# Low part of the attention rows and the last residual on GpSimd, means subtracted as they are: a macaron block on one Trainium2 core

## The chip, the cores and the metric

The kernel runs on one core of one Trainium2 chip. A core has five engines that work side by side, each through its own queue of instructions in order: TensorE (PE, with its weight loads shown apart as PEld), VectorE (DVE), ScalarE (ACT), GpSimd (POOL) and SyncE (SP), which here issues the DMAs. The metric is the device time of one execution in microseconds; lower is better. The time before is the median of three executions.

## The reference

One "macaron" layer on x of shape 8 x 1024 x 256: half a feed-forward block, an attention with relative positions (16 heads of 16 channels), and the same half feed-forward block again, each on a layer-normalized input and added to x.

```python
x = x + 0.5 * ffn(layernorm(x))
x = x + attention(layernorm(x))      # with a relative shift of the positions
x = x + 0.5 * ffn(layernorm(x))

def ffn(x):        return tanh(x @ W1 @ W2 @ W3 + bias)
def attention(x):
    content = einsum('bihd,bjhd->bhij', q + u_bias, k)
    pos     = relative_shift(einsum('bihd,jhd->bhij', q + v_bias, p))
    attn    = softmax((content + pos) * scale)
    return (attn @ v) @ Wo + bo
```

The change touches the layer norms (the mean that is subtracted) and the last two lines of work: the projection by Wo and the second feed-forward block.

## The kernel before

**Prologue** (to about 300 us). For each of eight groups of 128 positions it normalizes x, runs the first feed-forward block and computes queries, keys and values. The class Stats holds the statistics: ends() aggregates mean and variance on VectorE, negates the mean into a tile n (L272) and makes the reciprocal deviation r on GpSimd (rsqrt, L105 and L106); apply() (L287) computes (x + n) * r on GpSimd.

**Attention loop** (to about 2850 us). The scores are cut into 64 units: four groups of query rows by 16 heads. A unit has 16 steps, one for each of its query rows; a unit's sums over the values (L971, 128 matmuls) stand at the start of the next. step(T) writes out by hand the order in which each engine gets its work:

- TensorE: the first half of the scores of step T+2 (L1029), the subtraction of the maximum for step T (L959), a third of the second half (L1037), the transposed maxima of step T+1 (L945), the rest of the second half (L1043).
- VectorE: the maximum over each half (L934, twice), the two merged (L940: two f16 tiles of SBUF), the maximum over rows (L947).
- ScalarE: the exponentials of both halves (L963, twice), and a diagonal tile dg that holds the row maxima for L959 (L952).
- GpSimd: one copy a step (L225) that rearranges queries for the next unit, 16 for a unit. They are not paced: GpSimd takes them as soon as its queue reaches them and their tiles are free. The first of a unit waits until TensorE has read the tile for the last time.

PSUM holds three buffers of each half of the scores.

**Output work inside the loop.** When the 16 heads of a group of rows are done, the eight batches of that group are put through post_ops, one after the other, while the next group's scores run; so 24 of the 32 are done in the loop. posts(T) takes the next piece at the end of a step, and a number beside each piece says how many steps pass before the next one. The tiles of this use have one buffer (nb is 1). The pieces of one batch are: load; norm (GpSimd multiplies the heads' sums by the reciprocal denominators, L773); hi1 (ScalarE rounds num to f16 into the first part of hl, L777) and lo1 in the same step (what was lost by rounding, into the second part of hl, L780); projres one step later (12 matmuls with Wo, L786, and VectorE's residual, L798); ln (statistics and the negated mean, L112, L114, L117) and apply (GpSimd, L105, L106, L816) in one step; four steps later trans (L825, L830, L831); then ffn (L786, L837, and the tanh L838); fin (half of the tanh added to xr, L847); store. A batch takes exactly as many steps as a unit has, so each unit in such a stretch has one batch's pieces in the same places.

**The end** (from about 2850 us). The last group's eight batches go through post_ops with eight buffers (nb is 8) from ln on, staged by hand. There fin has two forms: for the first five batches ScalarE halves the tanh (L844) and GpSimd adds (L845); for the last three VectorE does both (L847).

Of the kernel before, what the change touches and what calls it, by code (L numbers as in the profile page):

```python
# [10 lines left out]
F32 = mybir.dt.float32  # L11
AF = mybir.ActivationFunctionType
ALU = mybir.AluOpType
# [3 lines left out]
P = 128  # L17
NB = 8
# [25 lines left out]
def macaron_kernel(  # L44
# [23 lines left out]
    nc = tc.nc  # L68
# [35 lines left out]
    def rsqrt(r, var):  # L104
        nc.gpsimd.tensor_scalar(r, var, 1.0, EPS, ALU.mult, ALU.add)  # L105
        nc.gpsimd.tensor_tensor(r, r, mhalf[:, : r.shape[1]], ALU.pow)  # L106

    def stats_dve(pool, xt, n, nm):
        st = pool.tile([P, n, 6], F32, tag="st" + nm, name="st" + nm)
        mv = pool.tile([P, n, 2], F32, tag="mv" + nm, name="mv" + nm)  # L110
        for b in range(n):
            nc.vector.bn_stats(st[:, b, :], xt[:, b, :])  # L112
        for b in range(n):
            nc.vector.bn_aggr(mv[:, b, :], st[:, b, :])  # L114
        r = pool.tile([P, n], F32, tag="r" + nm, name="r" + nm)
        nm_ = pool.tile([P, n], F32, tag="n" + nm, name="n" + nm)
        nc.vector.tensor_scalar_mul(nm_, mv[:, :, 0], -1.0)  # L117
        return nm_, r, mv

# [6 lines left out]
    class UnitSet:  # L128
        def __init__(self, pool, n):
            def t(name, shape):  # L130
                return pool.tile(shape, F16, tag=f"{name}{n}", name=f"{name}{n}")

            self.qc = t("qc", [KC, UT, 4, 32])
            self.q = t("q", [KR, UT + 1, NI * NB, 2])
            self.k = t("k", [KC, NI, 4, P])
            self.pg = t("pg", [KR, GW])
# [93 lines left out]
    if True:  # L230
        p2 = early.enter_context(tc.tile_pool(name="p2", bufs=2, side="right"))
# [25 lines left out]
        class Stats:  # L257
            def __init__(self, nm, xt):
                self.nm, self.xt = nm, xt
                self.st = p2.tile([P, NB, 6], F32, tag="st" + nm, name="st" + nm)  # L260
                self.mv = p2.tile([P, NB, 2], F32, tag="mv" + nm, name="mv" + nm)
                self.r = p2.tile([P, NB], F32, tag="r" + nm, name="r" + nm)
                self.n = p2.tile([P, NB], F32, tag="n" + nm, name="n" + nm)

            def rows(self, lo, hi):
                for b in range(lo, hi):
# [2 lines left out]
            def ends(self):  # L269
                for b in range(NB):  # L270
                    nc.vector.bn_aggr(self.mv[:, b, :], self.st[:, b, :])
                nc.vector.tensor_scalar_mul(self.n, self.mv[:, :, 0], -1.0)  # L272
                rsqrt(self.r, self.mv[:, :, 1])

            def again(self):
# [8 lines left out]
            def apply(self, tag):  # L284
                xn = p2.tile([P, NB, D], F32, tag=tag, name=tag, bufs=1)
                for b in range(NB):
                    nc.gpsimd.tensor_scalar(  # L287
                        xn[:, b, :], self.xt[:, b, :], self.n[:, b : b + 1],
                        self.r[:, b : b + 1], ALU.add, ALU.mult,
                    )  # L290
                return xn

# [125 lines left out]
        def key(xT, ks, m, h):  # L418
            ps = pst.tile([P, 512], F32, tag="t", name="kk")
            three(ps, wk16, xT, m, h)  # L420
            pv = ps.rearrange("p (b n) -> p b n", b=4)
            hi, lo = (ks[:, m, hl, 4 * h : 4 * h + 4] for hl in range(2))
            bc = bkk[:, m : m + 1]

            def one():
                nc.scalar.activation(hi, pv, AF.Identity, bias=bc)
                nc.vector.scalar_tensor_tensor(
                    out=lo, in0=pv, scalar=bc, in1=hi, op0=ALU.add, op1=ALU.subtract
                )

            return one
# [229 lines left out]
        for I in range(NI - 2, -2, -1):  # L661
# [39 lines left out]
            for n in range(4):  # L701
                q = query(xTb, cvst[(I + 1) % 2], n % 2, n // 2)
                k = key(xTb, ks, n % 2, n // 2)
# [24 lines left out]
    def load_rows(t, src, rg):  # L728
        for e, r in ((0, 16 * rg), (1, 64 + 16 * rg)):
            nc.sync.dma_start(  # L730
                t[:, e, :], src.rearrange("(k r) c -> k r c", r=P)[:, r : r + 16]
            )
# [21 lines left out]
    def post_ops(rg, b, sb, nb, pm, pt_, t):  # L754
        def new(name, shape, tag=None, dt=F32):
            t[name] = sb.tile(shape, dt, tag=tag or name, name=name, bufs=nb)
            return t[name]

        def load():
            num = new("num", [P, 2, 2 * P])  # L760
            den = new("den", [P, 2, 2 * P])
            for hh in range(2):
                hs = slice(8 * hh, 8 * hh + 8)
                nc.sync.dma_start(num[:, hh, :], h_d[rg, hs, 0:DH, b])
                nc.sync.dma_start(
                    den[:, hh, :],
                    r_d[rg, hs, b : b + 1, :].broadcast_to([8, DH, 2 * P]),
                )
            xr = new("xr", [P, 2, D])
            load_rows(xr, x1c_d[b], rg)  # L770

        def norm():
            nc.gpsimd.tensor_tensor(t["num"], t["num"], t["den"], ALU.mult)  # L773

        def hi1():
            new("hl", [P, 2, 2, 2 * P], dt=F16)
            nc.scalar.copy(t["hl"][:, 0], t["num"])  # L777

        def lo1():
            nc.vector.tensor_tensor(t["hl"][:, 1], t["num"], t["hl"][:, 0], ALU.subtract)  # L780

        def prod(ps, hl, w, tk, extra):
            n = 0
            for k in range(2):
                for a, c in ((0, 0), (1, 0), (0, 1)):
                    mm(  # L786
                        ps[:, tk, :], hl[:, a, k, tk * P : (tk + 1) * P], w[:, c, k, :],
                        start=n == 0, stop=n == 5 and not extra,
                    )
                    n += 1  # L790

        def proj():
            t["ps"] = pm.tile([P, 2, D], F32, tag=pt_, name="wops")
            for tk in range(2):
                prod(t["ps"], t["hl"], wo16, tk, False)

        def res():
            nc.vector.scalar_tensor_tensor(  # L798
                out=t["xr"], in0=t["ps"], scalar=1.0 / WS, in1=t["xr"], op0=ALU.mult,
                op1=ALU.add,  # L800
            )

        def projres():
            proj()
            res()

        def ln():
            if nb > 1:
                res()
            t["nm"], t["r"], t["mv"] = stats_dve(sb, t["xr"], 2, f"p{b % nb}")  # L810

        def apply():
            rsqrt(t["r"], t["mv"][:, :, 1])
            xn = new("pn", [P, 2, D])
            for k in range(2):
                nc.gpsimd.tensor_scalar(  # L816
                    xn[:, k, :], t["xr"][:, k, :], t["nm"][:, k : k + 1],
                    t["r"][:, k : k + 1], ALU.add, ALU.mult,
                )

        def trans():
            t["ps"] = pm.tile([P, 2, 2 * P], F32, tag=pt_, name="ptp")
            for c in range(2):
                for tk in range(2):
                    nc.tensor.transpose(  # L825
                        t["ps"][:, c, tk * P : (tk + 1) * P],
                        t["pn"][:, tk, c * P : (c + 1) * P], ident,
                    )
            new("pT", [P, 2, 2, 2 * P], "hl", F16)
            nc.scalar.copy(t["pT"][:, 0], t["ps"])  # L830
            nc.vector.tensor_tensor(t["pT"][:, 1], t["ps"], t["pT"][:, 0], ALU.subtract)  # L831

        def ffn():
            t["ps"] = pm.tile([P, 2, D], F32, tag=pt_, name="pff")
            for tk in range(2):
                prod(t["ps"], t["pT"], w16, tk, True)
                mm(t["ps"][:, tk, :], ones16, brow, start=False, stop=True)  # L837
            nc.scalar.activation(  # L838
                new("pth", [P, 2, D], "pn"), t["ps"], AF.Tanh, scale=1.0 / WS
            )  # L840

        def fin():
            if nb > 1 and b < NB - 3:
                nc.scalar.mul(t["pth"], t["pth"], 0.5)  # L844
                nc.gpsimd.tensor_tensor(t["xr"], t["xr"], t["pth"], ALU.add)  # L845
                return
            nc.vector.scalar_tensor_tensor(  # L847
                out=t["xr"], in0=t["pth"], scalar=0.5, in1=t["xr"],
                op0=ALU.mult, op1=ALU.add,
            )  # L850

        def store():
            store_rows(out[b], t["xr"], rg)

        return [
            (load, 4), (norm, 2), (hi1, 0), (lo1, 1), (projres, 0), (ln, 0), (apply, 4),
            (trans, 1), (ffn, 0), (fin, 1), (store, 1),
        ]

# [221 lines left out]
    num = [ttile(f"tn{k}", [P, NB, 2 * P]) for k in range(2)]  # L1081
# [152 lines left out]
```

## Time and profile before

| what | value |
|---|---|
| median of three executions | 2954.7 us (2951.74 to 2957.57) |
| the profiled execution | 2962.17 us, span of its profile 2960.5 us |
| granted TensorE clock, mean | 0.984; 1.00 through the loop |
| L934 (maxima), 2048 times | 687 ns each |
| L940 (merge of maxima), 1024 times | 224 ns at least, 226 median, 903 at most |
| L225 on GpSimd, two groups of 507 | 658 and 687 ns each |
| L780 (low part on VectorE), 24 times | 692 ns each |
| L773 (a product on GpSimd), 24 times | 1287 ns each |
| L845 (the addition on GpSimd), 5 times | 1267 ns median |
| L644 (a low part on GpSimd in the prologue), 4 times | 1155 ns each |

In the lines of the profile, out<-in names tiles, then come shapes and types, and a count. A line of the timeline begins with the start in us from the span's start and the time that the merged instructions took together; a bracket at its end is the time that the engine sat idle just before, with what ended that wait. A busy share over the whole span says little here, since the three stages have different limits; so the loop is read by units and steps.

### The profile page before, as it was taken

The page shows a single profiled execution, that of the slowest core. Times are in us where ns is not written, and L with a number is a line of the kernel's source. Part 1 is how long each engine was busy: PE and PEld are TensorE (multiplying, and loading weights), DVE is VectorE, ACT ScalarE, POOL GpSimd, SP SyncE. Part 2 cuts the span into 40 slices and gives each one's busy share as a digit, 9 for nine tenths or more (in the row PEclk, how much of TensorE's full clock was granted, in tenths as well). Part 3 has the DMA queues.
Part 4 walks back from the last instruction along what each step waited for, and adds up shares of the span by engine and source line. Part 5 has one row for each costly group of instructions (what it writes and reads, how often), then busy time and mean ns, then how long its engine had stood idle before and what let it go on. Part 6 is the DMA issues. An engine that isn't in the chain of part 4 may idle for free.

```text
span 2960.5 us, 157394 instructions
## 1 busy us (share of the span) xinstructions
PE 2835.1 (96%) x71212; PEld 2345.5 (79%) x71212; DVE 2188.1 (74%) x5001; ACT 1666.0 (56%) x3551; POOL 991.9 (34%) x1498
## 2 busy tenths in 40 slices
PE   7987999999999999999999999999999999999985
PEld 4755888888888888888888888888888888888874
DVE  7885777777777877877777787777777777777774
ACT  3655555555555655555555565556655556555552
POOL 8874222222222332332222332332222233232204
PEclk8999999999999999999999999999999999999997
DMA  4555322222223333322223323322223232222232
GB/s 146 185 164 177 87 69 68 65 66 67 67 68 76 85 85 86 85 76 68 66 66 78 84 81 86 83 70 70 70 70 78 82 87 81 83 68 65 67 88 70
DMA packets 333397, 250.63 MB, mean 85 GB/s; under 512 B 118885, under 2 KB 317142, under 8 KB 332246
## 3 DMA queue, kind: packets, MB, share of 16 engines
q1 hardware_dynamic: 332726, 240.56, 28.9%
q8 instruction: 558, 9.14, 1.3%
q14 instruction: 113, 0.93, 0.1%
HBM read 177.44 MB, written 62.78 MB: 81 GB/s over the span
## 4 chain that ended last, share of the span: by engine, by line
PE 83%; DVE 6%; DMA 2%; ACT 1%; issue 1%; SPq 1%; POOL 0%; ACTq 0%; DVEq 0%; POOLq 0%
PE s L1029 22%; PE s L1043 17%; PE av L971 15%; PE s L959 15%; PE s L1037 6%; DVE m L934 3%; PE mps L945 2%; PE pff L786 1%; DVE m L940 1%; PE wops L786 1%; DMA xr<-x1c_d 1%; ACT dg L952 1%; PE vv L467 1%; PE qq L454 1%; PE ptp L825 1%
## 5 line engine op out<-in xcount | busy, mean ns | idle before, releaser
L963 ACT ACTIVATE eT<-s 128x512 f32<-128x512 f32 x2048 | 1111.7, 594 | 992.3 <-PE s L959 990.7
L934 DVE TENSOR_REDUCE m<-s 128x128 f16<-128x512 f32 x2048 | 1406.3, 687 | 163.2 <-PE s L1029 30.6
L225 POOL TENSOR_SCALAR qc<-raw 48x256 f16<-48x256 f16 x507 | 328.6, 658 | 1229.0 <-PE s L1043 1191.4
L959 PE MATMUL s<-dg,many 128*128 128x512 f16 x2048 | 607.9, 378 | 33.0 <-ACT dg L952 33.0
L947 DVE TENSOR_REDUCE nm<-mps 128x1 f32<-128x128 f32 x1024 | 296.0, 289 | 450.3 <-PE mps L945 446.7
L1029 PE MATMUL s<-qc,k 114*128 114x32 f16 x16384 | 564.9, 176 | 18.9 <-DMA k<-c_d 18.9
L1037 PEld LDWEIGHTS <-k 114*128 114x128 f16 x8192 | 354.6, 96 | 244.3 <-issue 0.8
L1029 PEld LDWEIGHTS <-k 114*128 114x128 f16 x16384 | 487.9, 96 | 20.5 <-issue 19.1
L1029 PE MATMUL s<-q,pg 112*128 112x64 f16 (+3 forms) x12288 | 482.1, 184 | 0.5 <-issue 0.5
L1043 PE MATMUL s<-q,pg 112*128 112x64 f16 (+3 forms) x12288 | 481.7, 184 | 0.0
L971 PE MATMUL av<-eT,vt 128*32 128x256 f32 x8192 | 460.6, 382 | 19.8 <-DMA vt<-v_d 19.3
L952 ACT ACTIVATE dg<-ident,nm 128x128 f16<-128x128 f16 x1024 | 411.9, 402 | 77.0 <-DVE nm L947 66.4
L971 PEld LDWEIGHTS av<-eT,vt 128*32 128x32 f32 x8192 | 319.9, 139 | 133.6 <-issue 22.4
L1029 PEld LDWEIGHTS <-pg 112*128 112x128 f16 x12288 | 407.2, 97 | 0.6 <-issue 0.6
L1043 PEld LDWEIGHTS <-pg 112*128 112x128 f16 x12288 | 406.9, 97 | 0.0
L1037 PE MATMUL s<-qc,k 114*128 114x32 f16 x8192 | 364.5, 177 | 0.0
L1043 PE MATMUL s<-qc,k 114*128 114x32 f16 x8192 | 363.8, 177 | 0.0
L225 POOL TENSOR_SCALAR q<-raw 48x256 f16<-48x256 f16 x507 | 342.9, 687 | 20.1
L1043 PEld LDWEIGHTS <-k 114*128 114x128 f16 x8192 | 312.2, 96 | 0.0
L940 DVE TENSOR_TENSOR m<-m,m 128x128 f16<-128x128 f16 x1024 | 272.7, 266 | 35.2
L945 PE MATMUL mps<-ident,m 128*128 128x128 f16 x1024 | 222.5, 217 | 6.9 <-DVE m L940 4.5
L959 PEld LDWEIGHTS <-many 128*128 128x128 f16 x2048 | 127.3, 96 | 61.6 <-issue 61.2
(173 smaller groups left out, 1771.8 us busy)
## 6 DMA issues: line engine op xcount, KB each, us to landing
k<-k_d SPq DMA_DIRECT2D x128, 256.0 KB
vt<-v_d SPq DMA_DIRECT2D x128, 256.0 KB
raw<-qv_d SPq DMA_DIRECT2D x128, 144.0 KB
pg<-g_d SPq DMA_DIRECT2D x128, 132.5 KB
k<-k_d SPq DMA_DIRECT2D x128, 128.0 KB
h_d<-avs SPq DMA_DIRECT2D x126, 128.0 KB
qv_d<-cv SPq DMA_DIRECT2D x32, 288.0 KB
raw<-qv_d SPq DMA_DIRECT2D x128, 72.0 KB
```

What stands on the lines that cost most here:

```text
L225: nc.gpsimd.tensor_scalar(dst, src, 1.0, 0.0, ALU.mult, ALU.add)
L934: nc.vector.tensor_reduce(n, s_t[T][c].rearrange("p (j c) -> p c j", c=P), AX.X, ALU.max)
L940: nc.vector.tensor_tensor(n, n, m_t[T], ALU.max)
L945: mm(ps, m_t.pop(T), ident16, start=True, stop=True)
L947: r = nc.vector.tensor_reduce(nm, ps, AX.X, ALU.max, negate=True)
L952: nc.scalar.activation(dg, ident16, AF.Copy, scale=nm)
L959: mm(ps, many16, bass.AP(dg.tensor, dg.offset, [list(dg.ap[0]), [0, 4], [1, P]]), start=False, stop=True, skip_group_check=True,)
L963: nc.scalar.activation(eT[:, 4 * c : 4 * c + 4, :, t, :], ps.rearrange("p (j b n) -> p j b n", j=4, b=NB), AF.Exp,)
L971: mm(av[32 * c : 32 * c + 32, q, :], vt[:, j, :, 4 * q + c], eT[:, j, 4 * q + c].rearrange("p t n -> p (t n)"), start=j == 0, stop=j == NI ...
L1029: f()
L1037: f()
L1043: f()
```

## The change

Three edits in one.

- The negated mean is no longer made. stats_dve() and Stats hand on the mean as a view of the aggregate's tile, and the two appliers subtract it where they added: L117 and L272 disappear, one VectorE instruction for each set of statistics (32 and 16 times).
- lo1 in the loop moves from VectorE to GpSimd (24 times). The end of the kernel does not use lo1.
- fin in the loop takes the other form: ScalarE halves the tanh in place and GpSimd adds it to xr (24 times). At the end nothing changes: five batches go this way, three on VectorE, as before.

On each queue the pieces keep their places: lo1 stands on GpSimd's queue between the third and the fourth of a unit's query copies, the addition between the eleventh and the twelfth; ScalarE's multiplication stands behind the dg of its step. TensorE's and SyncE's instructions are the same and in the same order; the second weight load of the projection waits for GpSimd in place of VectorE, and so does the store.

```diff
@@ stats_dve
         r = pool.tile([P, n], F32, tag="r" + nm, name="r" + nm)
-        nm_ = pool.tile([P, n], F32, tag="n" + nm, name="n" + nm)
-        nc.vector.tensor_scalar_mul(nm_, mv[:, :, 0], -1.0)
-        return nm_, r, mv
+        return mv[:, :, 0], r, mv
@@ class Stats
-                self.n = p2.tile([P, NB], F32, tag="n" + nm, name="n" + nm)
+                self.n = self.mv[:, :, 0]
...
-                nc.vector.tensor_scalar_mul(self.n, self.mv[:, :, 0], -1.0)
                 rsqrt(self.r, self.mv[:, :, 1])
...
                         xn[:, b, :], self.xt[:, b, :], self.n[:, b : b + 1],
-                        self.r[:, b : b + 1], ALU.add, ALU.mult,
+                        self.r[:, b : b + 1], ALU.subtract, ALU.mult,
@@ post_ops
         def lo1():
-            nc.vector.tensor_tensor(t["hl"][:, 1], t["num"], t["hl"][:, 0], ALU.subtract)
+            (nc.vector if nb > 1 else nc.gpsimd).tensor_tensor(t["hl"][:, 1], t["num"], t["hl"][:, 0], ALU.subtract)
...
                     xn[:, k, :], t["xr"][:, k, :], t["nm"][:, k : k + 1],
-                    t["r"][:, k : k + 1], ALU.add, ALU.mult,
+                    t["r"][:, k : k + 1], ALU.subtract, ALU.mult,
...
         def fin():
-            if nb > 1 and b < NB - 3:
+            if nb == 1 or b < NB - 3:
                 nc.scalar.mul(t["pth"], t["pth"], 0.5)
                 nc.gpsimd.tensor_tensor(t["xr"], t["xr"], t["pth"], ALU.add)
                 return
```

## The prediction

> **What bounds the kernel now.** The page comes first: TensorE is busy almost all the time, VectorE three quarters of it, GpSimd a third.
>
> ```profile
> PE 2835.1 (96%) x71212; PEld 2345.5 (79%) x71212; DVE 2188.1 (74%) x5001; ACT 1666.0 (56%) x3551; POOL 991.9 (34%) x1498
> ```
>
> So a change on VectorE pays only where TensorE waits for it. The next view is the table of stretches for two units of the attention loop, one with a batch of output work in it and one without. (Columns: stretch, its length, busy time of PE, PEld, DVE, ACT, POOL, clock, DMA.)
>
> ```profile
> 995.80:1039.20 43.40, 42.20 (x1106) 35.58 (x1102) 32.85 (x74) 24.88 (x53) 13.78 (x21) 1.00 0.29 83
> ...
> 1376.50:1414.80 38.30, 38.30 (x1077) 32.33 (x1074) 28.36 (x65) 22.51 (x50) 10.54 (x17) 1.00 0.25 68
> ```
>
> A unit without output work has no TensorE gap at all: no edit can shorten it. A unit with one batch is 5.10 us longer and has gaps. There are 24 of these (L780 runs 24 times), so the timeline of one, TensorE's rows, tells nearly the whole story.
>
> ```profile
> 1015.89 0.59 PE L959 MATMUL s<-dg,many 128*128 128x512 f16 x2
> ...
> 1018.66 0.59 PE L959 MATMUL s<-dg,many 128*128 128x512 f16 x2 [0.68 <-ACT dg L952]
> ...
> 1020.61 0.59 PE L959 MATMUL s<-dg,many 128*128 128x512 f16 x2
> ...
> 1021.56 0.23 PE L945 MATMUL mps<-ident,m 128*128 128x128 f16 x1 [0.17 <-DVE m L940]
> ...
> 1022.88 0.59 PE L959 MATMUL s<-dg,many 128*128 128x512 f16 x2
> ...
> 1033.33 0.59 PE L959 MATMUL s<-dg,many 128*128 128x512 f16 x2 [0.27 <-ACT dg L952]
> ```
>
> L959 starts once a step, and an undisturbed step is 1.95 us (1013.95 to 1015.89). The brackets understate what is lost, because matmuls overlap; the distance of starts does not. (a) 1015.89 to 1018.66 is 2.77: 0.82 lost, after the statistics of the batch. (b) 1020.61 to 1022.88 is 2.27: 0.32 lost. (c) the next start is 1025.56, 2.68 later, of which the four transposes are 0.47 (1024.35 to 1024.82): 0.26 lost. (d) 1030.97 to 1033.33 is 2.36: 0.41 lost. Together 1.81 a batch, 43 us in 24 batches; the other 3.3 of the 5.10 are matmuls that stay. VectorE's rows say what each was.
>
> ```profile
> 1017.22 0.17 DVE L117 TENSOR_SCALAR np<-mvp 128x2 f32<-128x2 f32 x1
> 1017.29 0.69 DVE L934 TENSOR_REDUCE m<-s 128x128 f16<-128x512 f32 x1
> ...
> 1020.79 0.71 DVE L940 TENSOR_TENSOR m<-m,m 128x128 f16<-128x128 f16 x1
> ...
> 1023.07 0.63 DVE L940 TENSOR_TENSOR m<-m,m 128x128 f16<-128x128 f16 x1
> ...
> 1031.16 0.22 DVE L940 TENSOR_TENSOR m<-m,m 128x128 f16<-128x128 f16 x1
> 1031.30 0.68 DVE L847 SCALAR_TENSOR_TENSOR xr<-pth,xr 128x512 f32<-128x512 f32 x1
> ```
>
> A step has 0.69 + 0.29 + 0.69 + 0.22 = 1.89 us of VectorE work in 1.95, so anything added makes the maxima late. (a) is the statistics with L117 at their end; (d) is L847. In (b) and (c) L940, 0.22 us when alone, takes 0.71 and 0.63: it is held while GpSimd copies query tiles.
>
> ```profile
> 1018.35 1.11 POOL L816 TENSOR_SCALAR pn<-xr,np,rp 128x256 f32<-128x256 f32 x2
> 1019.43 1.99 POOL L225 TENSOR_SCALAR q<-raw 48x256 f16<-48x256 f16 x3
> 1021.51 2.85 POOL L225 TENSOR_SCALAR qc<-raw 48x256 f16<-48x256 f16 x4
> ```
>
> L940 at 1020.79 ends (1021.50) when the third copy has ended (1021.42), and the fourth starts only then (1021.51): the two take turns.
>
> **The change, part by part.** *The negated mean (L117, L272).* L117 leaves 32 times. The maximum behind it starts 0.09 before L117 ends at 1017.39; behind the second aggregate (end 1017.18) it would start at 1017.09, so (a) loses 0.20 of its 0.82. GpSimd's apply only reads another operand, and the power before it (L106) starts from the same aggregate, so pn does not move. In the prologue L272 leaves 16 times at 0.17, once at 3.56 (at 145.94, beside GpSimd's memsets), behind which TensorE waits 1.32 for L378 (row at 149.58). Bounds there: nothing, if the memset holds the neighbours too, to 1.9 (1.32 and 0.59 of waits) plus 15 x 0.17: 4.4. I take 1.3, the wait that stands directly behind it. In the last batches L117 goes 8 times (0.17 to 0.40), but GpSimd's own 2.25 us a batch (2928.85, 2931.10, 2933.35) keeps pace: 0 to 2, taken 0.5.
>
> *The low part (L780) to GpSimd.* VectorE gives up 0.69, but TensorE's projection behind it (1011.91 to 1013.22, 1.31) already hides that: no gap stands there, so the gain is nothing. The price is new: the projection's second weight load reads the low part. The high part ends on ScalarE at 1011.04 (1010.42 + 0.62). GpSimd needs some 0.08 to start behind another engine (aggregate end 1017.18, L105 at 1017.27) and 1.16 for the same shapes (L644 in the prologue): 1012.28, 0.06 more for TensorE (1021.50 to 1021.56), 1012.34. That load is due at 1011.92: **0.42 lost**. Bounds: 0.30 if the start costs nothing, 0.6 with the 1.29 of L773. Behind it on GpSimd's queue wait two copies, then the power, not due before 1017.27; no L940 falls into its 1.16 us (they start at 1010.87 and 1012.8).
>
> *The residual (L847) to ScalarE and GpSimd.* VectorE gives up 0.68 and (d), 0.41, goes. ScalarE gains one multiplication of 0.62 (L844): like L777 it starts 0.29 behind dg (1030.41), so it runs 1030.70 to 1031.32, in the 0.57 that ScalarE is idle before eT at 1031.39: hidden; without the cover eT would be up to 0.62 late, on tiles with three buffers. GpSimd adds from 1031.40 to 1032.67 (L845, 1.27). SyncE's queue reaches the store only at 990.02 in the first batch, 1.46 behind the end of L847 (987.88 + 0.68); the addition ends 0.69 behind it (1032.67 against 1031.98): no wait for the store, nor for the paced query load behind it. In the last batches nothing moves here: five already went this way.
>
> *What queues behind the addition.* After pn GpSimd ran eleven copies back to back; now six, then it waits for the addition, then five. The six: because (a) shrinks, VectorE arrives 0.20 earlier against them, near 1020.59, when the second copy (0.65 each) has about 0.1 to 0.2 left, rather than 0.6. From the rows, L940's hold costs TensorE its excess less 0.16 (0.49 gives 0.32, 0.41 gives 0.26), so up to 0.3 left of a copy is free. (b) goes, 0.32. Then the next L940 comes at 1022.5, with about 0.26 left of a copy: (c) goes too, 0.26. The five: from 1032.67 on, ends near 1033.3, 1034.0, 1034.7, 1035.3; undisturbed L940s arrive at 1033.10 and 1035.05, with 0.2 left each: free. Each of these four holds is bounded by 0 and 0.35 (a whole 0.65 left). The copies' deadline, the next unit's first scores near 1034.1 with the first of the five done at 1033.3, holds.
>
> A rule weighed here: the Trainium skill, "GPSIMD Engine Reference", section 1, says that GpSimd shares its SBUF interfaces with VectorE and that VectorE instructions with two SBUF inputs contend; L940 is one, and its 0.71 agrees. Taken as a penalty whenever GpSimd runs, it would make both halves of the copies cost as (b) and (c) do, and the sum that of the slower rival. The same page, section 3.1, has GpSimd 1.96 times slower in an elementwise addition; the rows give 1.16 to 0.69, 1.67 times. By the page's ratio the low part would take an estimated 1.35, 0.19 more a batch, 4.6 us in all.
>
> *The sum.* Per batch 0.42 - 0.20 - 0.32 - 0.26 - 0.41 = -0.77; 24 of them -18.5; prologue -1.3, end -0.5: **-20.3 us**. The profiled execution took 2962.2 (span 2960.5), so 2941.9 there; the runs' median, 2954.7, lies 7.5 below it, so I forecast **2934.4**.
>
> **The rivals.** *Holds by chance.* The meeting of L940 and copies may not be where I place it. With what is left of a copy anywhere in 0 to 0.65, a hold costs on average 0.35 x 0.35 / (2 x 0.65) = 0.09; four cost 0.38. Then -0.39 a batch, -9.4, with -1.8 outside: 2943.5. For it: 0.2 us of phase decide; against it: all 24 batches repeat the same times.
>
> *Port contention, slower.* The six copies hold L940 as now and the five do the same: 2 x 0.58 in place of my nothing, +0.39 a batch, +9.4 - 1.8 = +7.6: 2962.3. It decides from holds of 0.77 + 1.8/24 = 0.85 a batch on. For it: three L940s running are caught now; against it: each is caught just after a copy began, which the 0.20 shift undoes.
>
> *It comes to nothing.* The low part is late by 0.6 and two holds stay (0.58): 0.6 - 0.20 - 0.41 + 0 = -0.01 a batch, with -1.8 in all: 2952.9. Freed VectorE time then only becomes waiting.
>
> **How the numbers follow.** My forecast (2930 to 2939 with the bounds of the low part and the prologue) 0.52, chance holds 0.24, nothing 0.10, slower 0.14. A measurement tells 0.2%, 5.9 us, from no change; the first two lie on the faster side with little spill. The range 2930 to 2953 leaves out the slower rival and a little below. Faster 0.77, same 0.10, slower 0.13.
>
> **What would show it.** Units with a batch of about 42.65 instead of 43.4. Per step: a gap of some 0.4 inside the projection, waiting for GpSimd's low part; (a) near 0.62; L940 not above 0.3 us in all four places; no gap where (d) was. I am wrong if the projection waits longer than 0.6, or if L940's mean in these units stays at 0.3.

## The result, and the profile after

The changed kernel takes 3005.98 us in the median (3002.68 to 3007.96), against 2956.14 for the kernel before in the same set of runs: a ratio of 1.0174, with an interval from 1.0157 to 1.0191. It is 50 us slower, where 20 us faster was forecast. Its profiled execution took 3005.97 us, span 3004.3.

The page of the kernel after, its busy times:

```profile
PE 2856.8 (95%) x71212; PEld 2352.1 (78%) x71212; DVE 2154.4 (72%) x4905; ACT 1673.4 (56%) x3575; POOL 1177.8 (39%) x1546
```

VectorE is 34 us less busy, as it should be. GpSimd is 186 us busier, where the moved work is only about 59 (24 times 1.16 and 1.28). The next view, the table of stretches, says where. The first two rows are the prologue and the other two a unit with a batch and one without. (Columns: stretch, its length, busy time of PE, PEld, DVE, ACT, POOL, clock, DMA.)

```profile
0.00:100.00 100.00, 67.02 (x358) 43.84 (x359) 57.27 (x161) 29.26 (x48) 88.65 (x109) 0.83 0.37 117
100.00:300.00 200.00, 170.97 (x1099) 112.54 (x1098) 142.24 (x390) 97.35 (x164) 192.35 (x195) 0.91 0.48 152
1043.20:1086.10 42.90, 42.21 (x1109) 35.65 (x1105) 31.49 (x71) 25.12 (x54) 17.56 (x23) 1.00 0.30 84
1382.10:1420.40 38.30, 38.30 (x1079) 32.45 (x1077) 28.33 (x65) 22.48 (x50) 10.55 (x17) 1.00 0.25 68
```

The same first two stretches in the kernel before:

```profile
0.00:100.00 100.00, 79.33 (x468) 53.93 (x469) 73.21 (x217) 38.94 (x66) 80.35 (x132) 0.90 0.49 153
100.00:300.00 200.00, 170.61 (x1181) 113.10 (x1178) 144.69 (x394) 109.28 (x180) 136.73 (x196) 0.93 0.57 177
```

The loop did get faster: a unit with a batch went from 43.4 to 42.9 us, and one without stayed at 38.3. The prologue got slower: GpSimd is now busy for 192 of 200 us, where it was 137, though it runs about as many instructions. The view of one line names them. First the appliers of the prologue before, then after, each with the lines of what waited for them (us in total, times), and the apply of the output work after (minimum, median, maximum in ns; then first and last start):

```profile
L287 POOL TENSOR_SCALAR xn<-xt,na,ra x64: 547/553/2032, 13.5 to 220.7; 128x256 f32<-128x256 f32 x64
L287 POOL TENSOR_SCALAR xm<-xt,nb,rb x64: 548/554/1081, 50.4 to 257.2; 128x256 f32<-128x256 f32 x64
...
  PEld tp L352: 8.9, 10
  PE tp L352: 6.3, 6
```

```profile
L284 POOL TENSOR_SCALAR xn<-xt,mva,ra x64: 1212/1219/2676, 13.1 to 273.5; 128x256 f32<-128x256 f32 x64
L284 POOL TENSOR_SCALAR xm<-xt,mvb,rb x64: 1213/1219/1788, 60.3 to 309.1; 128x256 f32<-128x256 f32 x64
...
  PEld tp L349: 47.0, 35
  PE tp L349: 38.1, 32
...
L813 POOL TENSOR_SCALAR pn<-xr,mvp,rp x64: 1217/1220/1225, 1023.2 to 2988.0; 128x256 f32<-128x256 f32 x64
```

One apply, 128 x 256 in f32, took 0.55 us with add and mult; with subtract and mult it takes 1.22. The prologue has 128 of them: 128 x 0.666 = 85 us more of GpSimd. It was busy 217 of the first 300 us; 217 + 85 = 302, so it became what bounds that stage. TensorE's transposes wait 38 us for it, where they waited 6, and the first sum over values (L971 before, L968 after) starts at 384.9 us instead of 336.7, 48.2 later:

```profile
L971 PE MATMUL av<-eT,vt x8192: 379/379/642, 336.7 to 2913.1; 128*32 128x256 f32 x200
```

```profile
L968 PE MATMUL av<-eT,vt x8192: 379/379/641, 384.9 to 2946.1; 128*32 128x256 f32 x200
```

By the first sums over values of the units, the stages moved by +48.2 (to the loop), -11.8 (62 units, all of it in the 24 with a batch) and +7.4 (from the last unit of the loop on): +43.8, the difference of the spans. The medians differ by 50; the profiled execution before was a long one (2962.17 us against a median of 2956.14). The end has 16 of the slow appliers, 10.7 us more of GpSimd.

TensorE's rows of one unit with a batch, after; L956 is what L959 was:

```profile
1058.10 0.59 PE L956 MATMUL s<-dg,many 128*128 128x512 f16 x2
...
1059.74 1.37 PE L783 MATMUL wops<-wo,hl 128*128 128x256 f16 x11 [0.16 <-POOL hl L777]
1061.69 0.59 PE L956 MATMUL s<-dg,many 128*128 128x512 f16 x2
1063.63 0.59 PE L956 MATMUL s<-dg,many 128*128 128x512 f16 x2
1066.18 0.59 PE L956 MATMUL s<-dg,many 128*128 128x512 f16 x2 [0.46 <-ACT dg L949]
1068.12 0.59 PE L956 MATMUL s<-dg,many 128*128 128x512 f16 x2
1070.07 0.59 PE L956 MATMUL s<-dg,many 128*128 128x512 f16 x2
1072.49 0.59 PE L956 MATMUL s<-dg,many 128*128 128x512 f16 x2
...
1077.91 0.59 PE L956 MATMUL s<-dg,many 128*128 128x512 f16 x2
1079.85 0.59 PE L956 MATMUL s<-dg,many 128*128 128x512 f16 x2
1081.88 0.59 PE L956 MATMUL s<-dg,many 128*128 128x512 f16 x2
1084.06 0.59 PE L956 MATMUL s<-dg,many 128*128 128x512 f16 x2
```

Read as before, by distances less the 1.95 of a free step and less the matmuls of the output work: the projection's step is 3.59 long where it was 3.26 (0.33 lost, waiting for the low part); the statistics' loss (a) is 0.60, was 0.82; (b) is gone (1070.07 - 1068.12 = 1.95); so is (c) (2.42, with 0.47 of transposes); so is (d) (1.94). New are 0.08 and 0.23 in the two steps after the addition. VectorE's merges of the maxima show whose those are; the second row is where (b) was, and the third and the fourth are where the next merges were held before:

```profile
1066.32 0.40 DVE L937 TENSOR_TENSOR m<-m,m 128x128 f16<-128x128 f16 x1
...
1068.30 0.23 DVE L937 TENSOR_TENSOR m<-m,m 128x128 f16<-128x128 f16 x1
...
1070.25 0.33 DVE L937 TENSOR_TENSOR m<-m,m 128x128 f16<-128x128 f16 x1
...
1072.19 0.59 DVE L937 TENSOR_TENSOR m<-m,m 128x128 f16<-128x128 f16 x1
...
1080.03 0.46 DVE L937 TENSOR_TENSOR m<-m,m 128x128 f16<-128x128 f16 x1
...
1082.06 0.63 DVE L937 TENSOR_TENSOR m<-m,m 128x128 f16<-128x128 f16 x1
```

GpSimd's rows beside them show the applies with the first copies, and the addition with the copies behind it:

```profile
1066.10 2.43 POOL L813 TENSOR_SCALAR pn<-xr,mvp,rp 128x256 f32<-128x256 f32 x2
1068.50 2.00 POOL L223 TENSOR_SCALAR q<-raw 48x256 f16<-48x256 f16 x3
1070.58 2.12 POOL L223 TENSOR_SCALAR qc<-raw 48x256 f16<-48x256 f16 x3
1078.40 1.28 POOL L842 TENSOR_TENSOR xr<-xr,pth 128x512 f32<-128x512 f32 x1 [5.70 <-issue]
1079.77 0.65 POOL L223 TENSOR_SCALAR qc<-raw 48x256 f16<-48x256 f16 x1
1080.49 2.96 POOL L223 TENSOR_SCALAR q<-raw 48x256 f16<-48x256 f16 x4
```

### The profile page after: what moved, and what is told of

It reads as the page before. It is cut to its first block, busy times and chain, and to the rows that moved or that the text cites. A ratio compares the mean times of both kernels' runs of the same rounds, so it can differ in the third digit from the quotient of the medians.

```text
span 3004.3 us, 157362 instructions
## 1 busy us (share of the span) xinstructions
PE 2856.8 (95%) x71212; PEld 2352.1 (78%) x71212; DVE 2154.4 (72%) x4905; ACT 1673.4 (56%) x3575; POOL 1177.8 (39%) x1546
## 4 chain that ended last, share of the span: by engine, by line
PE 78%; POOL 10%; DVE 4%; DMA 2%; ACT 2%; issue 1%; SPq 1%; POOLq 0%; DVEq 0%
PE s L1026 22%; PE s L1040 16%; PE av L968 15%; PE s L956 14%; PE s L1034 6%; POOL xm L284 3%; POOL xn L284 2%; PE mps L942 2%; DVE m L931 2%; PE pff L783 1%; PE wops L783 1%; POOL hl L777 1%; DVE m L937 1%; POOL xt L381 1%; ACT eT L960 1%
## 5 line engine op out<-in xcount | busy, mean ns | idle before, releaser
L956 PE MATMUL s<-dg,many 128*128 128x512 f16 x2048 | 609.3, 378 | 21.5 <-ACT dg L949 21.5
L968 PE MATMUL av<-eT,vt 128*32 128x256 f32 x8192 | 460.3, 382 | 8.5 <-DMA vt<-v_d 7.9
L968 PEld LDWEIGHTS av<-eT,vt 128*32 128x32 f32 x8192 | 318.2, 139 | 123.9 <-issue 11.9
L956 PEld LDWEIGHTS <-many 128*128 128x128 f16 x2048 | 125.9, 96 | 48.5 <-issue 47.9
```

The lines of the kernel that those rows point to most:

```text
L956: mm(ps, many16, bass.AP(dg.tensor, dg.offset, [list(dg.ap[0]), [0, 4], [1, P]]), start=False, stop=True, skip_group_check=True,)
L968: mm(av[32 * c : 32 * c + 32, q, :], vt[:, j, :, 4 * q + c], eT[:, j, 4 * q + c].rearrange("p t n -> p (t n)"), start=j == 0, stop=j == NI ...
```

## The experiments

Two questions were open. What makes an apply slow: the operation, or the scalar that is now read from a view of the aggregate's tile? And which part of the change did what in the loop?

**The operation or the view.** In the changed kernel, add takes the place of subtract in both appliers, nothing else.

```diff
-                        self.r[:, b : b + 1], ALU.subtract, ALU.mult,
+                        self.r[:, b : b + 1], ALU.add, ALU.mult,
...
-                    t["r"][:, k : k + 1], ALU.subtract, ALU.mult,
+                    t["r"][:, k : k + 1], ALU.add, ALU.mult,
```

> The changed kernel with add in place of subtract in both appliers, the scalar still read from the view of the aggregate; the mean is added instead of subtracted, so the normalized rows are wrong by twice the mean and their times alone are read. Theory 'operation' (GpSimd's tensor_scalar is slow with subtract and mult): the applies go back from 1.22 to 0.55 us, the loop starts near 337 us in place of 385, units with a batch keep their 42.9, and the time is 2938 to 2946. Theory 'view' (the scalar read from a strided view is slow): the applies stay at 1.22 and the time at 3006. Theory 'moves' (the two moved operations are what costs): 3006 too, with the loop starting near 337.

Measured: 2946.65 us against 2952.34 for the kernel before (ratio 0.9978, 0.9962 to 0.9994), 59 us less than the changed kernel, but less of a gain than expected: the interval is 2 to 11 us, and the 24 units with a batch, 42.95 each, account for 11. One line of its profile, the first apply:

```profile
L284 POOL TENSOR_SCALAR xn<-xt,mva,ra x64: 546/554/2034, 13.2 to 211.3; 128x256 f32<-128x256 f32 x64
```

The view costs nothing (it is read here, mva); the operation makes the loss. The loop starts at 326.9. Both other theories fall. In the first 100 us of the changed kernel the granted clock was 0.83 against 0.90 before; here it is 0.90 again, so the lower clock came with the slow applies and is not a second cause.

**Eight forms side by side.** In the kernel before, the eight batches of the prologue's apply each get a form of their own (o, i: the tiles; n, r: columns of the negated mean and of r).

```diff
-                for b in range(NB):
-                    nc.gpsimd.tensor_scalar(
...
-                    )
+                g(o(0), i(0), n(0), r(0), ALU.add, ALU.mult)
+                g(o(1), i(1), n(1), r(1), ALU.subtract, ALU.mult)
+                g(o(2), i(2), self.mv[:, 2, 0:1], r(2), ALU.add, ALU.mult)
+                g(o(3), i(3), r(3), n(3), ALU.mult, ALU.add)
+                g(o(4), i(4), r(4), n(4), ALU.mult, ALU.subtract)
+                g(o(5), i(5), 0.25, 1.5, ALU.subtract, ALU.mult)
+                g(o(6), i(6), 0.25, 1.5, ALU.add, ALU.mult)
+                nc.gpsimd.tensor_scalar_mul(o(7), i(7), r(7))
```

> The kernel before, with eight forms of the prologue's apply on GpSimd, one for each of the eight batches, each 16 times on tiles of 128x256; the normalized rows of seven are not the layer norm's, so only durations are read. Theory 'operation': add and mult 0.55 us whether its scalar is a tile's column or the aggregate's view, subtract and mult 1.22 whether its scalars are columns or constants; whether mult and subtract is slow too is open. Theory 'view': the form with the view takes 1.22 and all others 0.55.

The lines of its profile, in the order of the diff (lines 289 to 296), half of the calls each:

```profile
L289 POOL TENSOR_SCALAR xm<-xt,nb,rb x8: 548/554/1059, 53.3 to 260.2; 128x256 f32<-128x256 f32 x8
L290 POOL TENSOR_SCALAR xm<-xt,nb,rb x8: 1223/1229/1735, 53.9 to 260.7; 128x256 f32<-128x256 f32 x8
L291 POOL TENSOR_SCALAR xm<-xt,mvb,rb x8: 550/554/868, 55.1 to 261.9; 128x256 f32<-128x256 f32 x8
L292 POOL TENSOR_SCALAR xm<-xt,rb,nb x8: 554/560/561, 55.6 to 262.4; 128x256 f32<-128x256 f32 x8
L293 POOL TENSOR_SCALAR xm<-xt,rb,nb x8: 1222/1230/1744, 56.2 to 263.0; 128x256 f32<-128x256 f32 x8
L294 POOL TENSOR_SCALAR xm<-xt x8: 1072/1076/1144, 57.4 to 264.2; 128x256 f32<-128x256 f32 x8
L295 POOL TENSOR_SCALAR xm<-xt x8: 397/399/404, 58.4 to 265.2; 128x256 f32<-128x256 f32 x8
L296 POOL TENSOR_SCALAR xm<-xt,rb x8: 922/929/1349, 58.8 to 265.6; 128x256 f32<-128x256 f32 x8
```

Same tiles, same shapes, same place in the kernel: the pairs of add and mult take 0.55 in either order, those with subtract 1.23 in either order, and with constants it is 0.40 against 1.08, 0.68 apart like the pairs with columns (0.67 and 0.68). A lone multiplication by a column takes 0.93, more than a multiplication and an addition together. Four of the eight forms are slow here, 2.1 us more for a whole apply, 34 us in all, and the loop starts at 342.3 us: 5.6 later than in the profile of before, and 11 to 15 later than in five other kernels with its prologue (327.5 to 331.3). So most of 34 us fits into GpSimd's idle time in the prologue, and 85 does not.

**The moves alone, and the mean alone.** The kernel before with a part of the edits: first the low part and the residual moved (the diff), then only the mean subtracted as it is (with the slow form).

```diff
-            nc.vector.tensor_tensor(t["hl"][:, 1], t["num"], t["hl"][:, 0], ALU.subtract)
+            (nc.vector if nb > 1 else nc.gpsimd).tensor_tensor(t["hl"][:, 1], t["num"], t["hl"][:, 0], ALU.subtract)
...
-            if nb > 1 and b < NB - 3:
+            if nb == 1 or b < NB - 3:
```

> The kernel before with the two moves alone (low part and residual), the negated mean kept on VectorE. Theory 'operation': nothing of the 50 us remains; from the loop's sums the low part's wait costs 0.33 a batch, the residual's gap gives 0.41 back, the five later copies cost 0.31, and the holds of 0.32 and 0.26 stay because nothing shifts their phase: +0.23 a batch, 2959 to 2964. Rival 'moves carry the loop's gain': the 0.55 a batch of the changed kernel comes from the moves, 2940 to 2946. Rival 'moves cost': near 3006.

Measured: 2960.48 against 2952.34, ratio 1.0026 (1.0009 to 1.0043), units with a batch 43.7: as the sum of the parts had it. Nothing of the 50 us is in it.

> The kernel before with the mean edit alone. Theory 'operation' or 'view': the prologue is 48 us longer and the end 7 us, as in the changed kernel; in the loop L117's 0.2 a batch goes, and if the longer apply moves the copies to where they hold nothing, 0.58 more: 2998 to 3014. Theory 'moves': below 2956.

Measured: 3002.34 against 2952.34, ratio 1.0153 (1.0127 to 1.0179). The loop starts at 389.1 us, and units with a batch take 42.6, the shortest so far. So the one edit holds both the loss, in the prologue and at the end, and the gain, in the loop.

**The mean as it is, in the loop alone.** stats_dve gets a flag; the prologue and the end keep the negated mean and the add.

```diff
+        if not negate:
+            return mv[:, :, 0], r, mv
         nm_ = pool.tile([P, n], F32, tag="n" + nm, name="n" + nm)
...
-                    t["r"][:, k : k + 1], ALU.add, ALU.mult,
+                    t["r"][:, k : k + 1], ALU.add if nb > 1 else ALU.subtract, ALU.mult,
```

> The kernel before, with the mean subtracted as it is only in the loop's 24 batches (GpSimd's slow form there, where it has idle time); prologue and end keep the negated mean and the fast form, and nothing is moved. Theory 'operation, and parts that add up': a unit with a batch falls from 43.41 to 42.62 us as in the run with the mean edit alone (0.22 of the statistics' wait, 0.33 and 0.25 of the holds), prologue and end as before: 17 to 19 us under the kernel before, 0.6%. Rival 'the slow form costs in the loop too': no change or slower.

Measured: 2937.07 against 2956.56, ratio 0.9925 (0.9901 to 0.9950), units 42.62. GpSimd has the time in the loop: its slow apply is hidden there.

**With the residual moved too.** The last kernel and the second line of the moves' diff (fin).

> The last kernel with the residual moved to ScalarE and GpSimd in the loop as well, the low part left on VectorE. Parts that add up: 0.41 given back, 0.31 lost to the five copies behind the addition: units with a batch 42.52, 19 to 22 us under the kernel before. Rival 'VectorE time freed is worth its length': 0.68 a batch more, 42.0 and 34 us under.

Measured: 2936.21, ratio 0.9931 (0.9908 to 0.9955), not to be told from the last one; units are 42.54, so 0.08 a batch or 2 us, as the parts add up and far from the rival's 42.0.

**The copies ahead of the addition.**

```diff
-            copy16(*preps.pop(0))
+            for _ in range(len(preps) if s == 10 else min(1, len(preps))):
+                copy16(*preps.pop(0))
```

> The last kernel with the unit's remaining query copies put on GpSimd's queue in step 10, ahead of the addition, so that none follows it. If the 0.31 is the five copies holding the merge of the maxima, it goes: units with a batch 42.2, 27 to 30 us under the kernel before, 0.9 to 1.0%. If the 0.31 belongs to the addition itself, units stay at 42.5.

Measured: 2925.65 against 2956.56, ratio 0.9897 (0.9874 to 0.9921), one per cent faster than the kernel before and the best of all. A unit with a batch in the table of stretches, and GpSimd's rows of that unit:

```profile
988.90:1031.10 42.20, 41.74 (x1106) 35.40 (x1103) 31.49 (x72) 25.05 (x54) 16.37 (x22) 1.00 0.32 87
```

```profile
1018.91 2.95 POOL L227 TENSOR_SCALAR q<-raw 48x256 f16<-48x256 f16 x4
1023.78 1.28 POOL L847 TENSOR_TENSOR xr<-xr,pth 128x512 f32<-128x512 f32 x1 [1.92 <-issue]
1026.28 0.65 POOL L227 TENSOR_SCALAR qc<-raw 48x256 f16<-48x256 f16 x1 [1.23 <-PE s L1045]
```

All the unit's copies are done (1021.86) before the addition starts; behind it stands only the next unit's first, and TensorE lost nothing in the steps after it. So the 0.31 was the copies behind the addition, not the addition itself.

**The low part alone.** The first line of the moves' diff.

> The kernel before with the low part alone moved to GpSimd. Parts that add up: its projection waits 0.33 for GpSimd and nothing is gained on VectorE: units with a batch 43.74, the loop 8 us longer. Rival 'VectorE time freed is worth its length': units of 42.7.

Measured in a single execution: 2960.07 us; units with a batch 43.75, and the projection waits for GpSimd:

```profile
1005.53 1.37 PE L786 MATMUL wops<-wo,hl 128*128 128x256 f16 x11 [0.15 <-POOL hl L780]
```

The move only costs, 0.34 a batch. What TensorE loses in a unit with a batch, read from the starts of its subtraction of the maximum in each kernel (us; "copies" are the two steps after the addition; a unit is the median of 24, from one first sum over values to the next):

| kernel | low part | (a) | (b) | (c) | (d) | copies | unit |
|---|---|---|---|---|---|---|---|
| before | 0 | 0.82 | 0.33 | 0.26 | 0.41 | 0 | 43.41 |
| after | 0.33 | 0.60 | 0 | 0 | 0 | 0.32 | 42.87 |
| after, with add | 0.33 | 0.60 | 0 | 0.08 | 0 | 0.33 | 42.95 |
| moves alone | 0.33 | 0.82 | 0.33 | 0.26 | 0 | 0.32 | 43.67 |
| means alone; in the loop alone | 0 | 0.60 | 0 | 0 | 0.41 | 0 | 42.62 |
| and the residual | 0 | 0.60 | 0 | 0 | 0 | 0.32 | 42.54 |
| and the copies first | 0 | 0.60 | 0 | 0 | 0 | 0 | 42.21 |
| low part alone | 0.33 | 0.82 | 0.33 | 0.26 | 0.41 | 0 | 43.75 |

## Why the prediction was wrong

The step that failed is "GpSimd's apply only reads another operand", with which the negated mean's edit was costed at nothing on GpSimd. The edit changes the operation too, from add to subtract, and that makes 192 instructions 0.67 us longer. The profile of before held no tensor_scalar with subtract on GpSimd, so the cost was unknown and had to be bounded from both sides; no bound was set, and so the range could not hold it. The subtractions of GpSimd in that trace are of two tensors; on 128 x 512 they take 1.16 (L644), no more than its addition (L845, 1.27), and the moved low part took 1.16 again: they would not have warned.

- *Prologue:* forecast -1.3, measured +48.2 by the start of the loop. What L272 gives back cannot be seen: with add in the changed kernel the loop starts at 326.9 us, and five other kernels, whose prologue is that of before, start it at 327.5 to 331.3, and the profile of before at 336.7. Against those five the changed kernel's loop starts 54 to 57 us late.
- *End:* forecast -0.5, measured +7.4. From the start of the last sums over values on it is +10.6 (57.5 to 68.1 us), near the 10.7 of the slow appliers; the unit before, which ends with a wait for a transfer, was 3.2 us shorter (62.5 to 59.3).
- *Loop:* forecast -18.5, measured -11.8; a unit with a batch became 0.54 shorter, not 0.77. The places were named rightly, and the table gives the terms. The low part's wait, 0.42 forecast, is 0.33: GpSimd's start (0.08), its 1.16 and TensorE's start (0.06) were as priced, but 1011.92 is when the projection's first matmul starts, and the load that waits belongs to the second, 0.11 later. (a) was to fall by 0.20 and falls by 0.22; (d) goes. (b) and (c) go too, but (c) with help that nobody forecast: the slow apply starts the copies 1.3 us later, and with add, at the forecast phase, (c) keeps 0.08.
- *The five copies behind the addition:* forecast free, measured 0.32, the term of the loop that was most mis-sized. The addition starts 0.13 us behind ScalarE's multiplication (1077.64 + 0.63, 1078.40), not 0.08; the first copy starts 0.09 behind the addition, not at once; and the copies then start some 0.73 apart (2.96 for four), where the forecast had 0.67. So the first merge finds 0.39 of a copy left and the second 0.55, not 0.2 each. What such a hold costs was priced rightly: 0.46 and 0.63 less the usual 0.22 and less 0.16 give 0.08 and 0.25, measured 0.08 and 0.23. The spacing could be read before: four copies took 2.85 there, each 0.08 behind the last, whether a merge ran between them or not. So "the two take turns" holds for the merge, which ends 0.07 to 0.08 behind the copy, and not for the copy.
- *The signs:* L940 was to stay under 0.3 us in four places and took 0.23, 0.33, 0.46 and 0.63; its mean in the units with a batch, which at 0.3 was to refute the forecast, is 0.31 before and after. It is a poor sign: five merges of a unit run long after, three before, but the one at 1072.19 (0.59) costs TensorE nothing: its step is 3.47 us long, and 3.48 with add, where that merge takes 0.23.
- *The rivals:* none named the prologue. In the loop the first one came nearest, with 0.38 a batch for four holds where 0.32 was measured, but not by its reason: all 24 batches repeat the same two holds (0.45 to 0.47 and 0.62 to 0.65). The slower one, 1.16 a batch for holds, did not occur in the changed kernel; the moves alone, which keep the old phase, lose 0.91 that way and are 0.26% slower.
- *The weighed rules:* a penalty for two inputs from SBUF whenever GpSimd runs is not what the rows show. Beside a copy the merge ends with it; beside the slow apply (two of 1.22 from 1066.10 on) it took 0.40 at 1066.32, and ended 0.60 before that apply did, in all 24 batches. Nor did the low part take the 1.35 that was weighed as an estimate: it took 1.16, as its row in the prologue said.

## What to carry to other kernels

An arithmetically equal form is not an equally fast one: where an edit changes an opcode on GpSimd, price that opcode with a row of its own or bound it, and multiply by all places that use it, in stages that the change was not meant for as well. In a kernel whose steps repeat, what an engine gives up is worth only the gap behind it: 0.69 us of VectorE moved in the projection's step was worth nothing, and 0.17 in the statistics' step was worth 0.73 (with add: 0.22 in (a), 0.33 in (b), 0.18 in (c)), as it also moved two merges out of the way of GpSimd. Side work that holds up another engine's instruction belongs where a slack covers it: putting the copies ahead of the addition was worth 0.33 a batch, where moving the residual had been worth 0.41 less 0.32.

## What was not expected of the hardware

GpSimd's instruction with two scalars takes 0.55 us on 128 x 256 in f32 with add and mult in either order, 1.23 with subtract and mult, and 0.93 for a lone multiplication by a column; with constants 0.40 and 1.08. In the profile of before, a multiplication by a column and by a constant in one instruction (L570) takes 0.47 to 0.49, half of the lone one. The Trainium skill, "GPSIMD Engine Reference", section 4.1, calls elementwise work of one input on GpSimd roughly line-rate; the rows differ by a factor of two and more from one pair of operations to the other, and here the measurement decides. What in the engine makes the difference no run shows.

The parts of the loop add up to within some 0.03 us of a unit in all eight rows of the table, even though they interact through the phase of two engines' instructions.
